# Two attention and mixture layers on one core: where one batch's shared expert and token sort stand among the next batch's attention units

## The chip, the cores and the metric

The kernel runs on one core of one Trainium2 chip. The core has a matrix engine (TensorE, PE in the profile, with its weight loads listed apart as PEld), a vector engine (VectorE, DVE), a scalar engine for activations (ScalarE, ACT), a general engine (GpSimd, POOL) and a queue engine (SyncE, SP) that issues most transfers. Each engine works through its own list of instructions in order and waits for the others by semaphores. The metric is the device time of one execution in microseconds (us); less is better.

## The reference, cut to what matters

Two batches `b` of 1,024 tokens with 128 channels go through two layers. Each layer adds an attention block and a mixture-of-experts block to the running sum `x`. All numbers are 32-bit floats. The change touches only the second layer's feed-forward block and its place beside the second layer's attention:

```python
logits = relu(xf @ Wr1 + br1) @ Wr2 + br2
tg, ti = top_k(softmax(logits), 2)
tg = softmax(tg / 2)
out = silu(xf @ Ws1 + bs1) @ Ws2 + bs2              # shared expert, every token
for e in range(8):                                  # routed experts
    h = silu(xf @ We1[e] + be1[e]) @ We2[e] + be2[e]
    w = sum(tg * (ti == e), axis=-1)
    out = out + w[:, None] * h
x = x + out
```

`xf` is the layer norm of `x` after the second attention. That attention is causal, with 16 heads of 8 channels, so a query tile with index `qt` (128 tokens) has only `(qt + 1) * 128` keys.

## The kernel before, in words

The first layer runs first, and then a short stretch in which the second layer's queries and keys of batch 0 are made. The second layer's attention is one loop over `N = 128` units `(b, qt, pr)`: batch, query tile, pair of heads. Units 0 to 63 are batch 0, units 64 to 127 batch 1, eight units (`pr`) to a query tile. In iteration `i` the loop issues, in this order: the scores of unit `i` (L1094 on PE; where this unit and the next are short, the scores and maxima of unit `i + 1` instead, one unit ahead), the transposes of the probabilities of `i - 1` (L1136), the exponentials of `i` (L1124 on ACT), the evictions of the transposes (L1142, on DVE and ACT), the product with the values for `i - 2` (L1175), at a tile's end the output projection (L1191), and then the side work. The negated maxima come from a DVE operation (L1102). A unit is short when it has at most 512 keys (`qt < 4`); its two heads then share one wide PSUM tile, and its maxima are taken in place. There are two wide PSUM tiles for scores, three banks (`bank()`) for everything else, and one accumulator.

PE, DVE, ACT and POOL keep the order in which the program issues, since this part is written under a manual schedule. So the place of a call in the loop is the place of its instructions in each engine's list.

The side work is written as generators that are advanced by one step at a time; a `yield` ends a step:

- `route1(b, t0, nt, ...)`, nine steps: statistics of the layer norm for `nt` tiles (L845, L846), the inverse root by a power on POOL (L108), one Newton step on DVE and four activations for the normed rows (L852), their transposes (L858), the copy to `lnT` (L859) and a write of the rows to `normed` in DRAM by SP, two router matmuls (L868, L873) with DVE operations between them, and three steps that pick the two largest gates (`picks`, small DVE operations).
- `send1(b, nt)`, twelve steps: the place of each token in an order sorted by expert, by prefix sums on PE and DVE (`places`), and then the token numbers for each sorted tile of 128 (`tokens_of`; sixteen accumulating matmuls at L357, a transpose at L363, and small DVE operations that end with the indices `s_id` at L375).
- `shared1(b, n)`, eight steps for 512 tokens, that is, two rounds of: a matmul of one quarter of the hidden width (L1056), its two activations (L1057 and the tanh L1059); the same for the next quarter, behind the DVE operation that ends the first (L1047); that operation for the second; eight products with the second weights (L1067) and the addition to `x` (L1069).
- `experts1(b, nt, early)`: the routed experts over sorted tiles. Its first step issues seven gathers on POOL (L923) by the indices of `send1`; the second asks for weights (L910, on SP); from the third on each step works on one tile (L962, L970, L975 on PE).

The list `side` holds pairs of a unit and a generator. `work(i)` advances the head of the list by one step, if its unit has come; a generator that has ended is dropped and the next one takes the step. The loop calls `work(i)` once at the end of each iteration, and once more from `last = 123` on. From unit 96 on, each odd iteration also advances `experts1` of batch 0. What is left of the list after the loop is done in the tail, with the rest of the experts, batch 1's shared expert and its own experts.

Of the kernel before, what the change touches and what calls it, by code (L numbers as in the profile page):

```python
# [23 lines left out]
NT = T // P  # L24
QB = 512
NQB = T // QB
TPB = QB // P
# [24 lines left out]
def two_layers(ctx, tc, a, out):  # L52
# [334 lines left out]
    with ExitStack() as st:  # L387
# [109 lines left out]
        N = len(units)  # L497
# [331 lines left out]
    def route1(b, t0, nt, tag_y, tag_n):  # L829


        if t0 == 0:
            y = a1.tile([P, T], F32, tag=tag_y, name="y1", bufs=1 if tag_y == "ckv" else 2)
            ys[b] = y.rearrange("p (t c) -> p t c", c=C)
            norms[b] = a1.tile([C, T], F32, tag=tag_n, name="lnT1", bufs=1 if tag_n == "lnT" else 2)
            gains[b] = small.tile([P, 2, NT], F32, tag="s_g", name="s_g", bufs=NB)
            hots[b] = small.tile([P, 2, NT, NE], F32, tag="s_h", name="s_h", bufs=NB)
        y, lnT = ys[b], norms[b]
        tiles = slice(t0, t0 + nt)
        cols = slice(t0 * P, (t0 + nt) * P)  # L840
        n = nt * P
        mv = small.tile([P, NT, 2], F32, tag="bnmv", name="bnmv", bufs=2)
        stats = small.tile([P, NT, 6], F32, tag="bnst", name="bnst", bufs=2)
        for t in range(t0, t0 + nt):
            nc.vector.bn_stats(stats[:, t, :], xs[b][:, t, :])  # L845
            nc.vector.bn_aggr(mv[:, t, :], stats[:, t, :])  # L846
        yield
        rstd = small.tile([P, NT], F32, tag="rstd", name="rstd", bufs=2)[:, tiles]
        yield from root(rstd, mv[:, tiles, 1], 2 if nt == 1 else 1)
        nm = shift(mv[:, tiles], rstd)  # L850
        for q in range(nt):
            nc.scalar.activation(y[:, t0 + q, :], xs[b][:, t0 + q, :], AF.Identity, bias=nm[:, q:q + 1],  # L852
                                 scale=rstd[:, q:q + 1])
        yield
        ps = bank()
        for q in range(nt):
            t = t0 + q
            nc.tensor.transpose(ps[:, q * P:(q + 1) * P], y[:, t, :], ident)  # L858
        nc.scalar.copy(lnT[:, cols], ps[:, :n])  # L859
        if nt > 1:  # L860
            nc.sync.dma_start(out=normed[b][t0 * P:(t0 + nt) * P, :].rearrange("(t p) c -> p t c", p=P),
                              in_=y[:, tiles, :])
        nc.gpsimd.tensor_tensor(xs[b][:, tiles, :], xs[b][:, tiles, :], bc(bs2.unsqueeze(1), [P, nt, C]), ALU.add)
        yield
        r1 = f1.tile([P, QB], F32, tag="r1", name="r1")
        nc.vector.memset(r1[32:33, :n], 1.0)
        ps = bank()
        nc.tensor.matmul(ps[:32, :n], wr1, lnT[:, cols], start=True, stop=True)  # L868
        nc.vector.tensor_scalar(r1[:32, :n], ps[:32, :n], br1, 0.0, ALU.add, ALU.max)
        yield  # L870
        ps = bank()
        for q in range(nt):
            nc.tensor.matmul(ps[:, q * NE:(q + 1) * NE], r1[:33, q * P:(q + 1) * P], wr2, start=True, stop=True)  # L873
        logits = small.tile([P, NT, NE], F32, tag="r_lg", name="r_lg", bufs=1)[:, :nt, :]
        nc.vector.tensor_copy(logits, ps[:, :nt * NE].rearrange("p (t e) -> p t e", e=NE))
        yield from picks(logits, nt, True, [hots[b][:, k, tiles, :] for k in range(2)],
                         [gains[b][:, k, tiles].unsqueeze(2) for k in range(2)])
        yield
# [193 lines left out]
    with ExitStack():  # L1072
        units = [(b, qt, pr) for b in range(NB) for qt in range(NT) for pr in range(8)]
        N = len(units)
# [121 lines left out]
        with tc.manual_schedule(engines={ET.PE, ET.DVE, ET.Activation, ET.Pool}):  # L1196
            steps = prepare(1)
            experts = experts1(0, NT, AHEAD)


            last = N // 2 + 8 * (NT - 1) + 3
            side = [(N // 2 + 3, route1(0, 0, TPB, "ckv", "lnT")), (0, route1(0, TPB, TPB, "ckv", "lnT")),
                    (0, send1(0, NT)), (0, shared1(0, 0)), (0, shared1(0, 1)),
                    (N // 2 + 8 * TPB + 3, route1(1, 0, TPB, "k0", "k1")),
                    (last, route1(1, TPB, 3, "k0", "k1")), (0, send1(1, NT - 1))]

            def work(i):

                while side and i >= side[0][0] and next(side[0][1], N) is not None:
                    side.pop(0)  # L1210

            issued = {}

            def issue(i):
                s = scores(i)
                issued[i] = maxima(i, s)

            for i in range(N + 3):
                ends = units[i - 1][:2] if 1 <= i <= N and units[i - 1][2] == 7 else None
                ahead = short(i) and short(i + 1)  # L1220
                if i < N and i not in issued:
                    if ahead:
                        issue(i)
                    else:
                        s = scores(i)
                if ahead:

                    issue(i + 1)
                if 1 <= i <= N:
                    probsT[i - 1] = a1.tile([P, 2 * NT, P], F32, tag="pT", name="pT", bufs=2)  # L1230
                    ps = fill(i - 1, 0)
                    if not short(i - 1):
                        for r in range(2):
                            evict(i - 1, 0, r, ps, nc.scalar.copy)
                if i < N:
                    if i in issued:
                        exponentials(i, *issued.pop(i))
                    else:
                        exponentials(i, *maxima(i, s))
                if 1 <= i <= N and short(i - 1):  # L1240
                    evict(i - 1, 0, 0, ps, nc.vector.tensor_copy)
                    evict(i - 1, 0, 1, ps, nc.scalar.copy)
                if ends:
                    recips[ends] = reciprocals(ends)
                if i >= last:
                    work(i)
                if 2 <= i <= N + 1:
                    values(i - 2)
                    if units[i - 2] == (0, NT - 1, 7):
                        spread_values(1)  # L1250
                if 1 <= i <= N and not short(i - 1):
                    ps = fill(i - 1, 1)
                    for r in range(2):
                        evict(i - 1, 1, r, ps, nc.vector.tensor_copy)
                probs.pop(i - 1, None)
                if i >= 3 and units[i - 3][2] == 7:
                    project_out(*units[i - 3][:2])
                work(i)
                if i >= N // 2 + 8 * TPB and i % 2:
                    next(experts, None)  # L1260
                if i < N:
                    b, qt, pr = units[i]

                    if b == 0 and qt >= 2 and (i % 2 or qt >= NT - 2) and (left > 6 or (qt, pr) >= (NT - 2, 3)):
                        next(steps, None)
                        left -= 1
                    if (b, qt, pr) == (0, NT - 1, 4):
                        for _ in steps:
                            pass
                    if qt + 1 < NT and pr == 0:  # L1270
                        mask_queries(b, qt + 1)
                    elif b + 1 < NB and (qt, pr) == (NT - 1, 5):
                        mask_queries(b + 1, 0)

            def run(*steps):

                return any([next(g, N) is None for g in steps])


            half, rest = shared1(1, 0), chain(route1(1, NT - 1, 1, "k0", "k1"), shared1(1, 1))  # L1280
            k = 0
            while side:
                work(N)
                if k % 2 == 0:
                    run(experts)
                run(rest)
                k += 1
            after = experts1(1, NT - 1, 1)
            for k in range(AHEAD):
                run(after)  # L1290
                run(half) if k % 2 else run(experts)
            while run(experts):
                run(after)
            combining = combine1(0, NT, 6)
            while run(after):
                run(half) or run(rest)
                run(combining)
            while run(half) or run(rest):
                pass
            dense, combining = all_experts1(1, NT - 1), combine1(1, NT - 1, 0)  # L1300
            while run(combining, dense):
                pass
            store(1, NT - 1, 1)
# [69 lines left out]
```

## Time and profile before

| what | value |
|---|---|
| median of three runs | 1475.38 us (1472.96 to 1479.55) |
| profiled execution | 1477.33 us, its span 1475.5 us |
| PE busy over the span | 1363.9 us (92%) |
| DVE, ACT, POOL busy | 1040.0 (70%), 905.2 (61%), 269.4 us (18%) |
| second attention, batch 0 (first exponential of unit 0 to that of unit 64) | 853.8 to 1055.5 us |
| batch 1, short units 64 to 95 | 1055.5 to 1148.5 us |
| batch 1, long units 96 to 119 | 1148.5 to 1280.1 us |
| units 120 to 127 and the tail | 1280.1 to 1475.5 us |

The table is read as follows. The profiled execution's own time is the span, in which its instructions lie, and 1.8 us around it. Busy times of engines overlap, so that they add up to far more than the span; what counts is which engine is busy nearly all the time in the stretch in question. The ends of matmuls are modelled. The stretches of the last four rows are cut at the first exponential (L1124) of a unit, found in the list of that line's instructions.

### The profile page before, as it was taken

What the parts mean: (1) busy time and instruction counts of PE and PEld (TensorE: products, weight loads), DVE (VectorE), ACT (ScalarE), POOL (GpSimd) and SP (SyncE); (2) the same over time, 40 slices, a digit from 0 to 9 for tenths busy, and PEclk for the clock granted to TensorE, in tenths of its full rate; (3) what the DMA queues carried; (4) which work ended last, traced back from release to release, by engine and by line L of the source; (5) the groups of instructions that cost most, each with busy time, mean ns of one, the idle gap of its engine ahead of it and who ended that gap; (6) DMA issues with size and microseconds to landing.
All of it is one profiled execution on the core that took longest, in us unless ns stands there. A gap on an engine that the chain in (4) does not pass through costs nothing.

```text
span 1475.5 us, 40490 instructions
## 1 busy us (share of the span) xinstructions
PE 1363.9 (92%) x16931; PEld 981.6 (67%) x16931; DVE 1040.0 (70%) x2376; ACT 905.2 (61%) x1915; POOL 269.4 (18%) x246
## 2 busy tenths in 40 slices
PE   5999999999999999999998989999987899987787
PEld 2777777777777776777765555666654577756676
DVE  3787767777766868777457478678879467877476
ACT  3778567777755776776422267867666577753443
POOL 1010010000000100000154641011021212213553
PEclk9999999999999999999999989999999999999999
DMA  4000000000000000000110030000000011112453
GB/s 111 2 16 17 16 2 17 16 16 17 16 16 2 16 16 16 17 16 2 31 35 1 0 92 2 2 2 2 2 16 30 16 30 34 50 30 66 140 128 112
DMA packets 31319, 43.15 MB, mean 29 GB/s; under 512 B 7545, under 2 KB 19506, under 8 KB 31138
## 3 DMA queue, kind: packets, MB, share of 16 engines
q1 hardware_dynamic: 25216, 28.47, 7.0%
q0 software_dynamic: 4352, 10.70, 2.8%
q8 instruction: 134, 2.20, 0.6%
q10 hardware_dynamic: 1570, 1.41, 0.4%
q14 instruction: 47, 0.39, 0.1%
HBM read 35.51 MB, written 5.05 MB: 27 GB/s over the span
## 4 chain that ended last, share of the span: by engine, by line
PE 77%; DVE 12%; ACT 6%; issue 4%; DMA 1%; another core or an unknown queue 0%; POOL 0%; DVEq 0%; POOLq 0%; SPq 0%; ACTq 0%
PE ps_s L507 16%; PE ps_a L574 16%; PE ps_t L557 10%; PE ps_s L1094 8%; PE ps_t L1136 4%; PE ps_s L253 3%; PE ps_a L1175 3%; DVE ps_s L1102 2%; PE ps_a L492 2%; PE ps_t L970 2%; PE ps_t L962 2%; PE ps_t L591 2%; ACT p L1124 2%; PE ps_t L728 2%; PE ps_t L263 2%
## 5 line engine op out<-in xcount | busy, mean ns | idle before, releaser
L516 DVE CUSTOM_DVE_ANT_0 p<-ps_s,zero 128x1024 f32<-128x1024 f32 x256 | 303.4, 1222 | 122.9 <-PE ps_s L507 121.8
L526 ACT ACTIVATE p<-p,nmx 128x1024 f32<-128x1024 f32 x256 | 293.1, 1153 | 6.7 <-DVE nmx L516 6.7
L563 ACT COPY pT<-ps_t 128x512 f32<-128x512 f32 x256 | 137.5, 589 | 199.3 <-PE ps_t L557 199.3
L507 PE MATMUL ps_s<-qk 64*128 64x512 f32 x1024 | 252.2, 607 | 1.5 <-DVE nmx L516 1.4
L574 PE MATMUL ps_a<-pT,zv 128*64 128x128 f32 x4096 | 251.8, 276 | 0.0
L574 PEld LDWEIGHTS ps_a<-pT,zv 128*64 128x64 f32 x4096 | 220.9, 137 | 9.3 <-issue 0.8
L557 PEld LDWEIGHTS ps_t<-ident,p 64*128 64x128 f32 x4096 | 160.3, 139 | 89.8 <-issue 85.9
L563 DVE COPY pT<-ps_t 128x512 f32<-128x512 f32 x256 | 164.9, 686 | 45.3 <-PE ps_t L557 43.1
L1094 PE MATMUL ps_s<-k,qm 64*128 64x512 f32 (+3 forms) x768 | 170.7, 533 | 13.6 <-ACT p L1124 11.2
L557 PE MATMUL ps_t<-ident,p 64*128 64x64 f32 x4096 | 178.1, 226 | 1.3 <-DVE pT L563 0.7
L1102 DVE CUSTOM_DVE_ANT_0 p<-ps_s,cmask 128x640 f32<-128x640 f32 (+3 forms) x128 | 126.0, 1022 | 71.2 <-PE ps_s L1094 60.8
L548 POOL TENSOR_TENSOR aoT<-aoT,recip 128x1024 f32<-128x1024 f32 x16 | 37.9, 2368 | 656.6 <-DMA recip<-flat 481.7
L507 PEld LDWEIGHTS ps_s<-qk 64*128 64x128 f32 x1024 | 93.2, 189 | 83.7 <-issue 74.7
L1142 ACT COPY pT<-ps_t 128x512 f32<-128x512 f32 (+3 forms) x192 | 95.7, 533 | 76.2 <-PE ps_t L1136 71.0
L1136 PEld LDWEIGHTS ps_t<-ident,p 64*128 64x128 f32 x2304 | 104.7, 140 | 55.6 <-issue 28.1
L1124 ACT ACTIVATE p<-p,nmx 128x640 f32<-128x640 f32 (+3 forms) x128 | 125.9, 992 | 4.5 <-DVE nmx L1102 4.5
L1136 PE MATMUL ps_t<-ident,p 64*128 64x64 f32 x2304 | 118.6, 228 | 9.3 <-issue 4.0
L1094 PEld LDWEIGHTS ps_s<-k,qm 64*128 64x128 f32 x768 | 71.7, 193 | 79.7 <-issue 43.6
L1175 PE MATMUL ps_a<-pT,vx 128*32 128x128 f32 x2304 | 98.3, 279 | 11.1 <-DVE pT L1142 10.2
L1142 DVE COPY pT<-ps_t 128x128 f32<-128x128 f32 (+3 forms) x192 | 87.3, 482 | 9.6 <-PE ps_t L1191 6.0
L1124 ACT ACTIVATE p<-ps_s,nmx 128x128 f32<-128x128 f32 (+3 forms) x128 | 66.3, 524 | 35.5 <-DVE nmx L1102 34.6
L899 ACT ACTIVATE th<-h 128x512 f32<-128x512 f32 x52 | 32.8, 630 | 87.9 <-DVE h L896 72.7
(255 smaller groups left out, 1817.2 us busy)
## 6 DMA issues: line engine op xcount, KB each, us to landing
we<-in_we SPq DMA_DIRECT2D x52, 256.0 KB
recip<-flat SPq DMA_DIRECT2D x32, 256.0 KB
we<-in_we POOLq DMA_DIRECT2D x1, 2048.0 KB
z<-results SPq DMA_DIRECT2D x6, 256.0 KB
x<-in_x SPq DMA_DIRECT2D x4, 256.0 KB
up<-in_up_proj POOLq DMA_DIRECT2D x1, 1024.0 KB
normed<-y SPq DMA_DIRECT2D x3, 256.0 KB
out_x<-x SPq DMA_DIRECT2D x3, 256.0 KB
```

The costliest lines, as they stand in the source:

```text
L507: nc.tensor.matmul(s[h][:, n * QB:(n + 1) * QB], qk[rows, 0, qt * P:(qt + 1) * P], qk[rows, 1, n * QB:(n + 1) * QB], start=True, stop=True)
L516: nc.vector.tensor_tensor_reduce(p, s, bc(zero, [P, T]), -1.0, 3e38, ALU.add, ALU.min, nmx)
L526: nc.scalar.activation(p, p, AF.Exp, bias=nmx, scale=-1.0, accum_out=ssum[:, h, qt:qt + 1])
L557: nc.tensor.transpose(ps[r][:, k * 64:(k + 1) * 64], probs[i][h][rows, k * P:(k + 1) * P], ident[rows, rows])
L563: copy(probsT[i][h][:, :, r * 64:(r + 1) * 64], ps[r].rearrange("p (j q) -> p j q", q=64))
L574: nc.tensor.matmul(acc[h * D0:(h + 1) * D0, cols], zv[:, j, :], probsT[i][h][:, j, :], start=(j == 0), stop=(j == NT - 1))
L1094: nc.tensor.matmul(s[h][:, n * QB:n * QB + w], qms[b, qt][rows, pr, :], kTs[b][pr // 4][rows, n * QB:n * QB + w], start=True, stop=True)
L1102: nc.vector.tensor_tensor_reduce(to[:, :nk], s[:, :nk], cmask[:, T - nk:], -1.0, 3e38, ALU.add, ALU.min, nmx)
L1124: nc.scalar.activation(p[:, h, :nk], s[h][:, :nk], AF.Exp, bias=nmx[h], scale=-1.0, accum_out=sums[b, qt][:, head:head + 1])
L1136: nc.tensor.transpose(ps[r][:, c * 64:(c + 1) * 64], probs[i][rows, h, j * P:(j + 1) * P], ident[rows, rows])
L1142: copy(probsT[i][:, 8 * f:8 * f + n, r * 64:(r + 1) * 64], ps[r][:, :n * 64].rearrange("p (j q) -> p j q", q=64))
L1175: nc.tensor.matmul(acc[to * 32:(to + 1) * 32, k * P:(k + 1) * P], vx[:, j, g, pr % 4 * 24:pr % 4 * 24 + 32], probsT[i][:, h * (qt + 1) + j ...
```

## The change

Two edits are made. In the list `side`, the two `shared1` of batch 0 move from behind `send1(0, NT)` to between and behind the two `route1` of batch 0, so that each half of the shared expert follows the routing of its own 512 tokens, and `send1` comes last of the five. And in iterations 64 to 95 each odd one calls `work(i)` a second time, so that three side steps are issued in two units, and not two.

```diff
-            side = [(N // 2 + 3, route1(0, 0, TPB, "ckv", "lnT")), (0, route1(0, TPB, TPB, "ckv", "lnT")),
-                    (0, send1(0, NT)), (0, shared1(0, 0)), (0, shared1(0, 1)),
+            side = [(N // 2 + 3, route1(0, 0, TPB, "ckv", "lnT")), (0, shared1(0, 0)),
+                    (0, route1(0, TPB, TPB, "ckv", "lnT")), (0, shared1(0, 1)), (0, send1(0, NT)),
                     (N // 2 + 8 * TPB + 3, route1(1, 0, TPB, "k0", "k1")),
                     (last, route1(1, TPB, 3, "k0", "k1")), (0, send1(1, NT - 1))]
...
                 work(i)
+                if N // 2 <= i < N // 2 + 8 * TPB and i % 2:
+                    work(i)
                 if i >= N // 2 + 8 * TPB and i % 2:
                     next(experts, None)
```

`NT` is 8 (tiles of 128 tokens in a batch) and `TPB` is 4 (tiles in 512 tokens), so `N // 2 + 8 * TPB` is 96 and `N // 2 + 8 * TPB + 3` is 99. No operation is added or taken away, and no buffer changes its size.

## The prediction

> **What bounds the kernel now.** I number the units of the second attention by the loop's `i`: batch 1 begins at 64, its short rows (128 to 512 keys) are 64 to 95, its long rows 96 to 127. The view of engine time by stretch comes first, cut where a unit's first exponential starts: batch 0's short units, batch 0's units 48 to 55, batch 1's short units (call it stage A), then batch 1's units 96 to 103 and 104 to 111 (together stage B), and 112 to 119.
>
> ```profile
> core 0: us, PE busy (x) PEld busy (x) DVE busy (x) ACT busy (x) POOL busy (x), PEclk, DMA share, GB/s
> 853.80:919.50 65.70, 58.63 (x776) 38.15 (x776) 52.09 (x192) 49.04 (x171) 17.85 (x25) 0.92 0.19 52
> 981.50:1020.90 39.40, 39.15 (x526) 23.58 (x522) 30.21 (x61) 25.24 (x51) 7.12 (x6) 1.00 0.01 2
> 1055.50:1148.50 93.00, 72.94 (x915) 48.29 (x911) 76.07 (x292) 52.00 (x183) 13.17 (x12) 0.96 0.06 19
> 1148.50:1191.90 43.40, 36.37 (x428) 23.52 (x424) 23.03 (x65) 28.48 (x64) 12.95 (x13) 0.92 0.09 24
> 1191.90:1235.50 43.60, 42.92 (x553) 31.20 (x552) 30.26 (x70) 32.13 (x70) 5.97 (x6) 1.00 0.11 32
> 1235.50:1280.10 44.60, 44.18 (x616) 33.17 (x614) 37.09 (x93) 31.66 (x70) 11.47 (x11) 1.00 0.15 45
> ```
>
> See PE: busy 72.94 of 93.0 us (0.78) in A, but 0.98 and 0.99 in the 44 us stretches from 1191.9 on. The chain of waits, asked for these stretches, says the same: adding up its listed pieces, A's chain lies 45.1 us on DVE and 24.3 on PE, B's 66.0 us on PE and 4.6 on DVE. So PE work taken out of B should shorten it; PE work put into A meets 20 us of idle PE, but behind DVE. Next the timeline of units 97 and 98, where B's first stretch falls to 0.84:
>
> ```profile
> 1153.94 1.12 PE L1056 MATMUL ps_t<-lnT,ws 128*128 128x512 f32 x2 [0.98 <-DVE recip L1182]
> ...
> 1160.95 1.07 ACT L1142 COPY pT<-ps_t 128x512 f32<-128x512 f32 x2 [4.59 <-remote]
> ...
> 1161.59 0.47 PE L1136 MATMUL ps_t<-ident,p 64*128 64x64 f32 x3 [3.77 <-issue]
> ...
> 1164.30 2.08 PE L1056 MATMUL ps_t<-lnT,ws 128*128 128x512 f32 x2 [1.00 <-DVE pT L1142]
> ```
>
> ACT stands 4.59 us before a copy whose matmuls had ended at 1156.84; PE then waits 3.77 us for the bank that this copy frees. All this lies inside seven gathers that POOL issues from 1152.36 to 1162.26. Afterwards the same pair of L1056 takes 2.08 us, not 1.12: from 1162.0 to 1168.5 the granted clock is 0.53. Cost by parts: 3.77 + 6.5 x (1 - 0.53) = 6.8; by units: 97 and 98 take 17.25 us between first exponentials, the neighbours 96 and 100 4.34 and 5.04, so 17.25 - 9.0 = 8.2. I take 7.5.
>
> **The change, part by part.** Before, one side step goes behind each unit from 67: nine of the first `route1`, nine of the second, twelve of `send1`, ending at 96, then batch 0's two `shared1` at 97 to 112. After, odd units up to 95 take two: 44 steps by 95, 46 by 97. Steps 1-9 are `route1` (67 to 72), 10-17 `shared1` (73 to 77), 18-26 `route1` (78 to 83), 27-34 `shared1` (84 to 89), 35-46 `send1` (89 to 97). Nothing is computed more or less.
>
> *What moves*: sixteen shared steps leave B for A. Their groups, of which batch 0 is half:
>
> ```profile
> L1056 PE MATMUL ps_t<-lnT,ws 128*128 128x512 f32 x32 | 19.4, 691 | 6.8 <-DVE x L1069 4.4 <-DVE pT L1142 1.0 <-DVE recip L1182 1.0
> L1067 PE MATMUL ps_t<-ws,hs 128*128 128x128 f32 x128 | 16.0, 278 | 0.3 <-ACT pT L1142 0.2
> L1067 PEld LDWEIGHTS ps_t<-ws,hs 128*128 128x128 f32 x128 | 14.9, 192 | 0.9 <-ACT pT L1142 0.9
> L1047 DVE SCALAR_TENSOR_TENSOR hs<-ths,hs 128x512 f32<-128x512 f32 x16 | 11.1, 693 | 0.0
> L1057 ACT ACTIVATE hs<-ps_t,bs 128x512 f32<-128x512 f32 x16 | 11.0, 686 | 4.9 <-PE ps_t L1056 4.1 <-issue 0.5
> ```
>
> PE: eight pairs of L1056 at 1.18 us (592 ns each at full clock) and four blocks of sixteen L1067 at 2.05 (1173.52 in the timeline) = 9.4 + 8.2 = 17.6 us. ACT: L1057 5.5 and L1059 5.5 = 11.0. DVE: L1047 5.5 and four L1069 at 0.69 = 8.3.
>
> *B without them*: -17.6 us. PE is left with about 58 us there (36.4 + 42.9 - 17.6, less the 3 us that the slow clock added), ACT with 60.6 - 11.0 = 49.6, DVE with 53.3 - 8.3 = 45, so PE stays the longest. "Perfetto Trace Analysis" of the Trainium skill (Identifying the Most-Contended Engine) speaks against this step: matmul busy time doesn't tell how loaded PE is, weight-load busy time does. By it B is loaded 0.54 and 0.72, the shared steps weigh (5.2 + 14.9) / 2 = 10.1 us (5.2 is L1056's own loads), and the sum below ends at -0.9. The trace settles it: from batch 0's units 48 to 55 to the same rows of batch 1 (39.40 us at 981.5, 44.60 at 1235.5; other side work stands there) the stretch grows 5.2 us, busy matmul 5.0, weight loads 9.6. The stretch follows matmul time; I take 17.6, and 10.1 as the weak end.
>
> *A with them*: the trace of before shows no shared step beside a short unit, so both ends. Best: PE 72.94 + 17.6 = 90.5 at the occupancy that batch 0's short units reach (58.63 / 65.70 = 0.89) gives 101.7, +8.7. Worst: nothing overlaps, PE, ACT and DVE parts add in full, 17.6 + 11.0 + 8.3 = +36.9. Between: the eleven units that carry shared steps are PE's. A short unit has 58.63 / 32 = 1.83 us of PE, so 20.1 + 17.6 = 37.7, at 0.95 (in paired steps the halving add L1047 stands at DVE's head until its tanh is there, and L1067 waits for that add) 39.7. The eighteen with `route1` and `send1` are DVE's: 52.09 / 32 = 1.63 us each, 29.3, and the steps' own 76.07 - 52.09 = 24.0, less one step, 23.2: 52.5 at A's own 0.82 is 64. Units 64 to 66: 6. Sum 109.7, **+16.7**. So I expect nearly no gain from A's idle PE, because the DVE steps that make it idle stand in other units than the matmuls.
>
> The weights that the shared steps need were asked at 858 to 859 us and the DMA is all but idle again by 890, so starting them at 73 waits for no transfer.
>
> *Two steps in one unit*: at 69 the wr1 matmul waits in PE's queue for the copy of `lnT` just asked of ACT, with the next scores behind it; at 79 the Newton step waits at DVE's head for POOL's power (1.0 us, row of L108), with the next maxima behind; at 81 the second router matmul waits for DVE. About 1 us each, held by the 0.82; below nothing if the pairs save a semaphore turn.
>
> *`send1` behind it*: the indices come one unit later (97, not 96), the gathers too. What needs them is the first expert transpose at 101: 0, at most +2. SP's gather source, `normed`, is written at 80 as before at 79.
>
> *Batch 1's first `route1`*: 113-121 before, 99-107 after (unit 98 has nothing due). PE about 4 us in either place (half of L858, L868, L873 in A), both at 0.98: 0, within 2. Its `normed` write passes ahead of five expert weight loads on SP's queue; its power stands behind seven gathers on POOL (1.25 us apart), done some 13 us after unit 97 starts, before 101 asks. 108 to 122 stay without a side step. From 123 on nothing moves.
>
> *The stall at 97*: ACT had run 1,725 instructions (its sequencer's counted). The 8,192-byte deliveries on the queue q14 `instruction` near ACT's earlier ones fall at counts 1213, 1341 and 1597, each a multiple of 128 from the others, and 1725 lies 128 behind the last; so ACT changed its code block in the midst of the gathers. After, sixteen more activations stand ahead of 97, the change comes about two units earlier, before the first gather, and the stall goes: -7.5. "Runtime: NRT & Kernel Launch" (Instruction fetch mechanics) says the opposite: crossing a block costs one tail bump, mostly hidden. Then the gathers alone stopped ACT and stop it again: 0. I go by the counts. With the stall gone, what is late next is PE itself.
>
> **Sum**: +16.7 - 17.6 - 7.5 = -8.4 us. The profiled execution took 1477.33 (span 1475.5 and 1.8 around it), 1.95 above the median 1475.38 of three; taken off that median: **1467**.
>
> **Rivals.** *The stall recurs*, or another engine's block change meets the gathers: -0.9, 1474.5. For: the burst is still there; against: the counts. *A absorbs*: +8.7 in place of +16.7, 1459. For: PE idle 20 us; against: A's chain on DVE. *Slower: ACT's and DVE's heads in the short units.* L1057 and L1059 stand in ACT's order ahead of the next unit's exponentials and must wait for L1056 behind the side matmuls; short units have two wide banks, so scores can run one unit ahead only. In A the list of waits has PE's loads for the scores standing for an exponential 9.5 us already, in 15 waits. If all of the 19.3 us of ACT and DVE work lies open: +36.9 - 17.6 - 7.5 = +11.8, **1487**; it outweighs the gains from 39% open ((25.1 - 17.6) / 19.3). Against: in B the same order leaves PE at 0.98. That the change doesn't do what it says is out: the built order has all sixteen steps ahead of unit 90.
>
> **Numbers.** Forecast 0.45 (its own range 1461 to 1472), stall recurs 0.23, A absorbs 0.12, slower 0.20. What a measurement tells from no change is 0.5%, 7.4 us. Faster: 0.12 + 0.45 x 0.7 = 0.44. Same: the rest of the forecast, most of the recurring stall and part of the slower case, 0.34. Slower 0.22. The range, 1455 to 1486, takes in all four but the outer tails.
>
> **What would show it.** Right: A near 110 us, PE about 0.83; B near 62, PE over 0.95, no ACT gap of 4 us and the clock at 1.0; unit 123 reached 8 us earlier. Wrong: A over 118, with ACT gaps before exponentials and PE stopped at L1094; B under 12 us shorter; a 4 us gap anew.

## The result and the profile after

The changed kernel takes **1489.47 us** (median of four, 1486.0 to 1491.99) where the kernel before takes 1476.64 (four runs, 1472.96 to 1479.55): ratio **1.0088, 95% interval 1.0061 to 1.0116**. The forecast was 1467, 0.6% faster. The profiled execution took 1486.0, its span 1484.2.

The view of engine time by stretch, cut at the same units as the one in the prediction: units 64 to 95 (stage A), 96 to 103 and 104 to 111 (stage B), 112 to 119.

```profile
core 0: us, PE busy (x) PEld busy (x) DVE busy (x) ACT busy (x) POOL busy (x), PEclk, DMA share, GB/s
1049.90:1167.50 117.60, 95.15 (x961) 60.36 (x958) 85.65 (x304) 61.19 (x198) 13.41 (x12) 0.83 0.05 15
1167.50:1208.50 41.00, 34.51 (x447) 24.66 (x438) 23.18 (x75) 25.73 (x62) 15.06 (x15) 0.92 0.12 32
1208.50:1247.50 39.00, 36.54 (x522) 28.42 (x522) 30.46 (x85) 27.40 (x64) 5.98 (x6) 1.00 0.11 36
1247.50:1288.80 41.30, 41.09 (x587) 30.76 (x585) 31.60 (x65) 29.60 (x63) 8.89 (x9) 1.00 0.14 42
```

A grew from 93.0 to 117.6 us, by 24.6 where 16.7 were forecast. B went from 87.0 to 80.0, by 7.0 where 25.1 were forecast, and PE is still free for 9 us of it. The last stretch gave 3.3: the last shared matmuls (unit 112) and batch 1's first `route1` have moved out of it. The shared steps cost PE the same as before: over the whole execution the L1056 matmuls take 18.9 us (19.4 before) and L1067 takes 16.5 (16.0).

A's list of groups shows where new waits stand. First the kernel before, then the changed one; the figures after the bar are busy us, mean ns of one, then the engine's idle time ahead of the group and who ended it.

```profile
L852 ACT ACTIVATE y<-x,shift,rstd 128x128 f32<-128x128 f32 x8 | 3.3, 482 | 2.5 <-DVE shift L119 2.5
L858 PE MATMUL ps_t<-ident,y 128*128 128x128 f32 x8 | 2.9, 402 | 1.5 <-ACT y L852 1.3
L869 DVE TENSOR_SCALAR r<-ps_t,br 32x512 f32<-32x512 f32 x2 | 1.5, 739 | 0.2 <-PE ps_t L868 0.2
```

```profile
L1047 DVE SCALAR_TENSOR_TENSOR hs<-ths,hs 128x512 f32<-128x512 f32 x8 | 6.0, 749 | 4.8 <-ACT ths L1059 4.8
L852 ACT ACTIVATE y<-x,shift,rstd 128x128 f32<-128x128 f32 x8 | 3.3, 482 | 7.3 <-DVE shift L119 7.3
L858 PE MATMUL ps_t<-ident,y 128*128 128x128 f32 x8 | 3.3, 475 | 3.5 <-ACT y L852 3.5
L1069 DVE SCALAR_TENSOR_TENSOR x<-ps_t,x 128x512 f32<-128x512 f32 x4 | 2.8, 692 | 4.1 <-PE ps_t L1067 4.1
L869 DVE TENSOR_SCALAR r<-ps_t,br 32x512 f32<-32x512 f32 x2 | 1.5, 739 | 3.9 <-PE ps_t L868 3.9
```

These are the same operations with the same durations, but each now stands at the head of its engine and waits for a result that was asked for just ahead of it: 4.8 us more at L852, 2.0 at L858, 3.7 at L869, and 8.9 new ones on DVE at the shared expert's L1047 and L1069.

The timeline at unit 98 shows the stop that the forecast had taken away:

```profile
1176.84 1.07 ACT L1142 COPY pT<-ps_t 128x512 f32<-128x512 f32 x2 [0.87 <-PE ps_t L1136]
1177.21 1.09 POOL L923 DMA_INDIRECT back<-normed,s_id  x1 [18.09 <-DVE s_id L375]
...
1179.79 0.66 PE L1136 MATMUL ps_t<-ident,p 64*128 64x64 f32 x16
...
1183.64 0.95 POOL L923 DMA_INDIRECT back<-normed,s_id  x1 [0.30 <-issue]
1184.89 0.95 POOL L923 DMA_INDIRECT back<-normed,s_id  x1 [0.30 <-issue]
1185.99 1.07 ACT L1142 COPY pT<-ps_t 128x512 f32<-128x512 f32 x2 [6.46 <-remote]
1186.63 0.47 PE L1136 MATMUL ps_t<-ident,p 64*128 64x64 f32 x3 [4.44 <-ACT pT L1142]
```

The copy on ACT needs the sixteen transposes that ended at 1180.45. It begins at 1185.99, just after the last of the seven gathers (1184.89 + 0.95 = 1185.84), and PE stands 4.44 us behind it. In the kernel before, ACT was let go at 1160.95, and the seventh of eight gathers (the forecast had counted seven up to 1162.26) ended at 1161.00; DVE stood 6.00 us at its own copy (L1142), until 1163.95. A second profile of the changed kernel has the same stop (6.40 and 4.39 us). In a second profile of the kernel before, ACT is let go after 3.20 us, during the sixth gather, and DVE stands 5.98 us.

### The profile page after: what moved, and what is told of

Read it like the earlier page. It is cut to its first block, busy times and chain, and to the rows that moved or that the text cites. A ratio compares the mean times of both kernels' runs of the same rounds, so it can differ in the third digit from the quotient of the medians.

```text
span 1484.2 us, 40479 instructions
## 1 busy us (share of the span) xinstructions
PE 1369.4 (92%) x16931; PEld 987.6 (67%) x16931; DVE 1042.5 (70%) x2376; ACT 904.9 (61%) x1915; POOL 268.6 (18%) x246
## 4 chain that ended last, share of the span: by engine, by line
PE 76%; DVE 11%; ACT 7%; issue 4%; another core or an unknown queue 1%; DMA 1%; POOL 0%; DVEq 0%; ACTq 0%; POOLq 0%; SPq 0%
PE ps_s L507 15%; PE ps_a L574 15%; PE ps_t L557 10%; PE ps_s L1094 8%; PE ps_t L1136 4%; PE ps_s L253 3%; PE ps_a L1175 3%; DVE ps_s L1102 2%; ACT p L1124 2%; PE ps_a L492 2%; PE ps_t L591 2%; PE ps_t L962 2%; PE ps_t L728 2%; PE ps_t L263 2%; PE ps_t L970 2%
## 5 line engine op out<-in xcount | busy, mean ns | idle before, releaser
L557 PEld LDWEIGHTS ps_t<-ident,p 64*128 64x128 f32 x4096 | 159.3, 139 | 89.1 <-issue 85.3
L563 DVE COPY pT<-ps_t 128x512 f32<-128x512 f32 x256 | 164.8, 685 | 44.4 <-PE ps_t L557 42.1
L1094 PE MATMUL ps_s<-k,qm 64*128 64x512 f32 (+3 forms) x768 | 173.2, 537 | 11.7 <-ACT p L1124 10.0
L557 PE MATMUL ps_t<-ident,p 64*128 64x64 f32 x4096 | 177.0, 225 | 1.3 <-DVE pT L563 0.7
L1142 ACT COPY pT<-ps_t 128x512 f32<-128x512 f32 (+3 forms) x192 | 96.0, 535 | 86.0 <-PE ps_t L1136 79.0
L1136 PEld LDWEIGHTS ps_t<-ident,p 64*128 64x128 f32 x2304 | 109.1, 144 | 56.7 <-issue 25.2
L1136 PE MATMUL ps_t<-ident,p 64*128 64x64 f32 x2304 | 123.9, 232 | 9.5 <-ACT pT L1142 6.1
L1094 PEld LDWEIGHTS ps_s<-k,qm 64*128 64x128 f32 x768 | 74.2, 195 | 75.0 <-issue 40.2
L1175 PE MATMUL ps_a<-pT,vx 128*32 128x128 f32 x2304 | 101.7, 284 | 13.6 <-DVE pT L1142 12.6
L1142 DVE COPY pT<-ps_t 128x128 f32<-128x128 f32 (+3 forms) x192 | 87.2, 482 | 12.8 <-PE ps_t L1136 12.4
```

The lines of the kernel that those rows point to most:

```text
L557: nc.tensor.transpose(ps[r][:, k * 64:(k + 1) * 64], probs[i][h][rows, k * P:(k + 1) * P], ident[rows, rows])
L563: copy(probsT[i][h][:, :, r * 64:(r + 1) * 64], ps[r].rearrange("p (j q) -> p j q", q=64))
L1094: nc.tensor.matmul(s[h][:, n * QB:n * QB + w], qms[b, qt][rows, pr, :], kTs[b][pr // 4][rows, n * QB:n * QB + w], start=True, stop=True)
L1136: nc.tensor.transpose(ps[r][:, c * 64:(c + 1) * 64], probs[i][rows, h, j * P:(j + 1) * P], ident[rows, rows])
L1142: copy(probsT[i][:, 8 * f:8 * f + n, r * 64:(r + 1) * 64], ps[r][:, :n * 64].rearrange("p (j q) -> p j q", q=64))
L1175: nc.tensor.matmul(acc[to * 32:(to + 1) * 32, k * P:(k + 1) * P], vx[:, j, g, pr % 4 * 24:pr % 4 * 24 + 32], probsT[i][:, h * (qt + 1) + j ...
```

## The experiments

Each kernel was compared with the kernel before on its own chip. Two chips served; on the second every kernel ran some 28 us faster (the kernel before 1447.05 there, about 1475 on the first), so only ratios and stretches are compared across them. Stretches are cut at the first exponential of a unit, in the profiled execution, and take in both units named; "half" is the time in which the granted clock was about 0.5.

| kernel | ratio (95%) | units 64-96 (half) | 97-103 | 104-122 |
|---|---|---|---|---|
| before, two profiles | 1 | 97.3 (6.8), 96.9 (13.7) | 39.1, 38.8 | 104.1, 104.2 |
| changed, two profiles | 1.0088, 1.0087 (1.0063-1.0111) | 124.3 (41.0), 126.1 (37.5) | 34.3, 34.3 | 96.0, 96.0 |
| single_routes | 1.007 (1.005-1.0091) | 119.8 (23.9) | 35.0 | 97.3 |
| after_warm | 1.0144 (1.0124-1.0164) | 128.9 (30.7) | 34.4 | 95.9 |
| before_gathers_apart | 0.9988 (0.9976-0.9999) | 99.8 (23.9) | 35.7 | 106.2 |
| pairs_alone, second chip | 1.0039 (1.0029-1.005) | 106.0 (41.0) | 30.8 | 103.5 |
| pairs_even, second chip | 1.0081 (1.0049-1.0112) | 107.3 (44.4) | 30.8 | 103.5 |
| after_spread, second chip | 1.0092 (1.006-1.0125) | 125.3 (41.0) | 25.9 | 96.5 |
| after_spread_again, first chip | 1.0077 (1.0048-1.0106) | 125.3 (41.0) | 29.3 | 97.9 |
| beside | 0.9978 (0.9963-0.9994) | 108.1 (13.7) | 34.1 | 95.9 |
| beside_spread, second chip | 0.9998 (0.9981-1.0016) | 107.7 (13.7) | 28.8 | 96.3 |
| beside_spread_again, first chip | 0.9955 (0.9939-0.9972) | 108.0 (13.7) | 29.3 | 97.6 |

### Is it the two steps in one unit, or the shared expert in short rows?

**The changed order, with single steps of the routing and the sort, and the shared expert in four packs.** Each `shared1` runs four steps in a unit, in units 76, 77, 87 and 88; the experts' odd units start at 101.

```diff
+            packed = (N // 2 + 12, N // 2 + 13, N // 2 + 23, N // 2 + 24)
...
-                if N // 2 <= i < N // 2 + 8 * TPB and i % 2:
-                    work(i)
-                if i >= N // 2 + 8 * TPB and i % 2:
+                if i in packed:
+                    for _ in range(3):
+                        work(i)
+                if i > N // 2 + 8 * TPB + 4 and (i % 2 or i < N // 2 + 8 * TPB + 10):
```

> The order of the changed kernel, but the steps of route1 and send1 stand one to a unit as before, and each shared1 is put whole into two units (four steps each, units 76, 77, 87, 88); send1 then ends at unit 100 and the routed experts begin at 101 and catch up by 109. Theory A (two DVE-heavy steps in one unit leave PE idle, and the granted clock halves): in units 64 to 100 the clock is halved for about 7 us, as before the change, not 41 us; the total is 8 to 12 us under the changed kernel, 1.001 to 1.004 of before. Theory B (shared1's matmuls and activations in short units cost this by themselves, at the heads of ACT's and DVE's queues): the total stays at 1.008 or above, as four shared steps in one unit are denser still.

Units 64 to 96 took 119.8 us, and the kernel stayed slower. The waits of `route1` went back to those of before (L869 0.2 us, L852 3.0), but those of the shared expert grew (L1047 6.3, L1069 9.1). So the pairs of routing steps are not the whole cause: shared steps in units of their own cost 22 us here, although four steps of `send1` had moved out behind unit 96. They stand four to a unit, as a chain of dependent steps; one to a unit, without other side work beside them, was not tried. Neither forecast came whole: the total was above the 1.004 of theory A and just under the 1.008 of theory B, and the half-clock time 23.9 us, not 7.

**The second step alone.** The list of before, with the second step in odd units up to 95 and the shared expert held back to unit 97, where it was.

```diff
-                    (0, send1(0, NT)), (0, shared1(0, 0)), (0, shared1(0, 1)),
+                    (0, send1(0, NT)), (N // 2 + 33, shared1(0, 0)), (0, shared1(0, 1)),
...
                 work(i)
+                if N // 2 <= i < N // 2 + 8 * TPB and i % 2:
+                    work(i)
```

> The kernel before, with the second step in each odd unit from 65 to 95 alone: route1, route1 and send1 end at unit 86 in place of 96, and batch 0's shared1 stays at units 97 to 112. Theory P (two dependent steps in one unit cost extra, whatever stands there): units 64 to 95 last 100 to 106 us, not 93.0, the clock is halved for more than 20 us of them, and the total is 1.004 to 1.009 of before. Theory S (the extra time of the changed kernel comes from shared1 in the short units, not from the pairs): units 64 to 95 last 90 to 95 us and the total is within 0.002 of before.

Units 64 to 96 took 106.0 us, 8.7 more than before: nothing was added, yet the thirty steps took 72.3 us in the twenty units 67 to 86, the ten units then left bare 26.4, and together 98.7 where the thirty units had taken 90.1 with one step each.

The extra lies in the routing. Its two `route1` took 20.8 and 22.6 us in six units each, where nine units had taken 22.9 and 24.8; `send1` took 28.9 us in eight units where twelve had taken 42.4. Batch 0's units of the same rows give a rough measure of what the units cost without these steps (an estimate from the profile of before, since other side work stands in some of them): over it the two `route1` cost 22.7 us here and 13.4 before, `send1` 11.3 and 10.6. The groups of units 64 to 95 show the waits:

```profile
L868 PE MATMUL ps_t<-lnT,wr 128*32 128x512 f32 x4 | 3.8, 1061 | 2.0 <-ACT lnT L859 2.0
L852 ACT ACTIVATE y<-x,shift,rstd 128x128 f32<-128x128 f32 x8 | 3.3, 481 | 6.5 <-DVE shift L119 6.5
L858 PE MATMUL ps_t<-ident,y 128*128 128x128 f32 x8 | 3.3, 475 | 2.0 <-ACT y L852 2.0
L869 DVE TENSOR_SCALAR r<-ps_t,br 32x512 f32<-32x512 f32 x2 | 1.5, 738 | 6.9 <-PE ps_t L868 6.9
```

**The same in even units.** Which two steps share a unit might matter, since in the changed kernel the second `route1` pairs a power on POOL with the Newton step that reads it, and one router matmul with the next. The edit is that of the run above with `i % 2 == 0`.

> The earlier run with the second step alone (in odd units 65 to 95) took 106.0 us over units 64 to 96 where the kernel before takes 97.3. Here the same second step stands in the even units 68 to 94, and nothing else differs. If any two steps in one unit cost the same, whichever they are, these units take 106 us again. If it is steps that depend on each other (in even units the pairs of the first and second route1 fall so that a step that raises a power on POOL and the Newton step on DVE that reads it, and a router matmul and the next, stand in one unit; in odd units of the earlier run they did not), they take 111 to 116 us.

Units 64 to 96 took 107.3 us: which steps are paired hardly matters. The waits only change places, as the same groups of this kernel show.

```profile
L852 ACT ACTIVATE y<-x,shift,rstd 128x128 f32<-128x128 f32 x8 | 3.3, 482 | 8.4 <-DVE shift L119 8.4
L858 PE MATMUL ps_t<-ident,y 128*128 128x128 f32 x8 | 3.3, 474 | 4.2 <-ACT y L852 4.2
L873 PE MATMUL ps_t<-wr,r 33*128 33x8 f32 x16 | 2.9, 304 | 1.8 <-DVE r L869 0.9 <-issue 0.9
L869 DVE TENSOR_SCALAR r<-ps_t,br 32x512 f32<-32x512 f32 x2 | 1.5, 738 | 0.9 <-PE ps_t L868 0.9
```

From 6.9 us at L869, the wait has gone to L852 and L858. (The two kernels' ratios differ by 0.4% although units 64 to 122 differ by 1.3 us only; in the profiles the rest lies ahead of unit 64, where the programs are the same, and behind 122.)

**The shared expert beside the routing.** Here the list keeps single steps, and each odd unit from 71 gets one shared step beside its routing or sorting step. `tile_hot` of `send1` gets a buffer of its own, as its slot was that of `hs`.

```diff
-        tile_hot = a1.tile([P, 2 * QB], F32, tag="hs", name="hot")[...]
+        tile_hot = a1.tile([P, 2 * QB], F32, tag="hot", name="hot")[...]
...
-                    (0, send1(0, NT)), (0, shared1(0, 0)), (0, shared1(0, 1)),
+                    (0, send1(0, NT)),
...
+            beside = chain(shared1(0, 0), shared1(0, 1))
...
                 work(i)
...
+                if N // 2 + 7 <= i and i % 2:
+                    next(beside, None)
```

> The list and the single steps of the kernel before, but batch 0's shared1 is taken out of the list and advanced by one step in each odd unit from 71 to 101, so that its matmuls share units with the DVE steps of route1 and send1 (the hot tile of send1 gets a buffer of its own). Theory A: the clock in units 64 to 95 is halved for 7 us or less, the short units last 100 to 106 us (93.0 before, 117.6 after), and the total is 0.990 to 0.999 of before. Theory B: the short units last 112 us or more, and the total is 1.005 or above.

Units 64 to 96 took 108.1 us with thirteen of the sixteen shared steps in them, and the kernel became faster than before, by 0.2% (95% interval 0.06 to 0.37). Its groups in units 64 to 95:

```profile
L1047 DVE SCALAR_TENSOR_TENSOR hs<-ths,hs 128x512 f32<-128x512 f32 x6 | 4.1, 684 | 0.0
L852 ACT ACTIVATE y<-x,shift,rstd 128x128 f32<-128x128 f32 x8 | 3.3, 481 | 2.8 <-DVE shift L119 2.8
L1069 DVE SCALAR_TENSOR_TENSOR x<-ps_t,x 128x512 f32<-128x512 f32 x3 | 2.1, 689 | 1.6 <-PE ps_t L1067 1.6
L869 DVE TENSOR_SCALAR r<-ps_t,br 32x512 f32<-32x512 f32 x2 | 1.5, 738 | 0.2 <-PE ps_t L868 0.2
```

Two steps share a unit here too, but they belong to two chains that don't depend on each other. The wait at L1047 is 0.0 where it was 4.8, and the routing's waits are close to those of the kernel before (2.8 and 0.2 us, 2.5 and 0.2 there).

### Is it the clock?

The clock stood at one half for 41 us of units 64 to 96 after the change, for 6.8 before. PE's work there is stretched by it: 95.15 us are busy in units 64 to 95 where 72.94 + 17.6 - 3.7 (L357 had moved to unit 96) = 86.8 were due.

**More work for PE.** The changed kernel, with the transposes of the probabilities (L1136) of batch 1's short units done twice.

```diff
-            for c, (h, j) in enumerate(blocks(i)[8 * f:8 * f + 8]):
+            for _ in range(2 if N // 2 <= i < N // 2 + 8 * TPB else 1):
+                for c, (h, j) in enumerate(blocks(i)[8 * f:8 * f + 8]):
...
```

> The changed kernel, with every transpose of the probabilities of batch 1's short units issued twice into the same place, some 15 us more of PE work without a wait of its own. Theory A (the halved clock is what costs): the clock in units 64 to 95 rises from 0.83 to 0.95 or more, and the total is no longer than that of the changed kernel, in spite of the work. Theory B (the clock only follows idle time that other waits make, and costs nothing): the short units last 8 to 15 us longer than the 117.6 us of the changed kernel.

The half-clock time only fell to 30.7 us, and the stretch grew to 128.9. Neither theory's figure came: the clock in units 64 to 95 rose to 0.88, not 0.95, and these units became 3.4 us longer, not 8 to 15, with 6.1 us more of busy PE. The stronger witness is the program of units 64 to 96 of before, which stands unchanged in three profiles (the third is that of before_gathers_apart, below): its half-clock time was 6.8, 13.7 and 23.9 us, its stretch 97.3, 96.9 and 99.8 us. From the first to the second a halved us costs nothing, from the first to the third 0.15 us, from the second to the third 0.28. At such rates, which are estimates from single profiles, the 41 - 7 us after the change would explain between nothing and 10 us of the 27. So the clock is not the whole cause, and its share stays open.

### What stops ACT at unit 97 or 98?

The forecast had put the stop down to a change of ACT's code block in the midst of the gathers. In the changed kernel the instruction delivery fell at 1163.95, when ACT had run 1,723 instructions, and the stop began at 1179.5, 15.6 us later, with ACT at 1,747. In the kernel before, the delivery itself fell at 1162.18, when ACT had already been let go. So that theory had fallen before any experiment. Nor does a delivery on the other queue of instructions, q8, make the stop by itself: there is one at 1177.00, just ahead of the first gather, and none from there to the stop's end; with the gathers held apart (below) one stands just as close (1182.84, first gather 1182.96), and there is no stop. What was left was the burst of gathers.

**The gathers one by one, in the kernel before.** `experts1` was told to issue one gather for each step, one step to a unit.

```diff
-            experts = experts1(0, NT, AHEAD)
+            experts = experts1(0, NT, 1)
...
-                if i >= N // 2 + 8 * TPB and i % 2:
+                if i >= N // 2 + 8 * TPB + 1 and (i % 2 or i < N // 2 + 8 * TPB + 14):
```

> The kernel before, with the seven first gathers of batch 0's routed experts issued one to a unit in units 97 to 103 and not all at 97; the experts' steps then go one to a unit up to 109, where they have caught up. Theory G (the burst of gathers holds up ACT's wait for PE): no gap over 3 us on ACT before L1142, the granted clock 1.0 in units 96 to 103, and 5 to 9 us less in all, 0.994 to 0.997. Theory C (it is ACT's change of code block that meets a gather, which is where I put it in the prediction): ACT's gap of 4 us stays, or moves, and the total is within 2 us of before.

The edit failed to do what it was for: nothing made POOL wait between the gathers, so that it ran ahead of the units and issued them 1.26 us apart as ever. The stop was there (3.21 us on ACT, 4.63 on DVE), and the run says nothing of the burst.

**The gathers held apart, in the changed kernel.** Ahead of each gather POOL adds two columns of the unit's maxima, and so has to wait for that unit.

```diff
-            experts = experts1(0, NT, AHEAD)
+            experts = experts1(0, NT, 1)
...
+                if N // 2 + 8 * TPB < i < N // 2 + 8 * TPB + 8:
+                    pace = small.tile([P, 1], F32, tag="pace", name="pace", bufs=1)
+                    nc.gpsimd.tensor_tensor(pace, moved[1][0], moved[1][0], ALU.add)
+                if i >= N // 2 + 8 * TPB + 1 and (i % 2 or i < N // 2 + 8 * TPB + 14):
...
```

> The changed kernel, with the seven first gathers held apart in time: ahead of each, in units 97 to 103, POOL adds up two columns that DVE writes in that unit, so that it cannot run ahead (in before_gathers_apart nothing held it, and the gathers still came 1.26 us apart). Theory G (the burst of gathers holds up what waits for PE): no gap over 2.5 us on ACT or PE in units 97 to 103, the clock 1.0 there, and 5 to 9 us less than the changed kernel, 1.003 to 1.006 of before. Rival: each gather holds up PE's release by itself, and seven small gaps take the place of the large one; the total is within 2 us of the changed kernel's.

> The changed kernel with the gathers held apart by POOL. Theory G: units 97 to 103 last 26 us on any chip; where after_again has its stop, 7 to 9 us less than after_again, where it has none, the same.

> The changed kernel, once more, on the same chip as its neighbours here. Units 64 to 96 last 124 us as before on either kind of chip (theory P: pairs and shared1 cost 27 us there). Units 97 to 103 last 34 us where the gathers stop PE, 26 to 27 where they do not; in the second case the total is still 1.007 to 1.010 of before, as before loses its own stop too.

> The kernel before, once more, for a profile on the same chip as the next three. If the stop at units 97 and 98 belongs to the burst of gathers on every chip: units 97 to 103 last about 39 us and ACT stands over 4 us before L1142. If it belongs to the chip of the first two calls, as pairs_alone suggests (the same burst, 30.8 us, no stop, on a chip where all kernels are 28 us faster): units 97 to 103 last 31 to 33 us wherever the total is near 1447 us, and 39 us wherever it is near 1475 us.

The first of these runs was on the second chip; the others are on the first, with both kernels unchanged among them. Its timeline there, at the same units:

```profile
1182.96 1.10 POOL L923 DMA_INDIRECT back<-normed,s_id  x1 [3.45 <-DVE s_id L375]
...
1184.46 0.98 POOL L923 DMA_INDIRECT back<-normed,s_id  x1 [0.16 <-issue]
...
1186.30 1.07 ACT L1142 COPY pT<-ps_t 128x512 f32<-128x512 f32 x2 [1.00 <-PE ps_t L1136]
...
1187.61 0.96 POOL L923 DMA_INDIRECT back<-normed,s_id  x1 [0.45 <-issue]
...
1189.53 1.07 ACT L1142 COPY pT<-ps_t 128x512 f32<-128x512 f32 x2 [0.54 <-PE ps_t L1136]
```

With 1.4 us and more from one gather to the next, ACT waits 1.00 us where it stood 6.46, and unit 98 takes 3.69 us in place of 9.16. Units 97 to 103 are 5.0 us shorter, but 104 to 122 are 1.9 longer, and the medians (1487.38 against 1488.72) don't tell the two apart; both held-apart runs of this order missed the totals expected of them (1.003 to 1.006 of before on the second chip, 7 to 9 us less than the changed kernel on the first). So, in this order and on this chip, the burst is needed for the stop, and the stop is worth 5 us where it stands; how much of it reaches the end can't be told.

The stop is not ACT's alone. In single_routes, on the first chip, the burst stands four units later, and there DVE waits for transposes that had ended at 1186.52, until 1.6 us after the last gather:

```profile
1186.19 0.33 PE L1136 MATMUL ps_t<-ident,p 64*128 64x64 f32 x3 [1.00 <-DVE nmx L1102]
...
1188.82 0.95 POOL L923 DMA_INDIRECT back<-normed,s_id  x1 [0.30 <-issue]
1191.34 0.49 DVE L1142 COPY pT<-ps_t 128x128 f32<-128x128 f32 x2 [5.56 <-remote]
```

In beside it is DVE again (4.70 us, until 1.5 us after the last gather). So every profile of a burst on the first chip has such a stop, on ACT, on DVE or on both.

On the second chip pairs_alone and pairs_even issued their gathers in a burst too, 1.25 us apart but from 6.7 us ahead of unit 97 on, and have no stop: units 97 and 98 of pairs_alone took 9.2 us, those of the kernel before 17.25 and 17.0 in its two profiles. Whether the chip or the earlier place of the burst makes that difference was not tried apart, and why ACT and DVE are let go so late after PE's matmuls in a burst stays open.

**Both together.** The shared expert beside the routing, and the gathers held apart: the edits of beside and after_spread in one kernel.

> The kernel beside, with the gathers held apart in the same way. Theory G: 3 to 8 us less than beside, 0.992 to 0.996 of before. Rival: the same as beside, 0.998.

> shared1 beside route1 and send1, and the gathers held apart. Where before has the stop: 0.991 to 0.996 of before. Where it has none: 0.998 to 1.001, as in the run on the faster chip.

On the first chip it took 1468.12 us where the kernel before took 1475.08, ratio 0.9955 (0.9939 to 0.9972): the best of all, and faster than both kernels. On the second chip it is even with before (0.9998), under the 0.992 to 0.996 that were expected; that the kernel before has no stop there would explain it, but no profile of it was taken on that chip. Its gain over beside (0.9978) is within the two intervals.

## Why the prediction was wrong

Between units 64 and 122 the forecast's sum was -8.4 us, and the profiles have 254.6 - 240.5 = +14.1 (in the profiled execution 5.6 of it was hidden, as unit 64 began earlier). The difference of 22.5 us divides by the forecast's own terms so:

- **The eighteen units with routing and sorting, 64 us.** They took 20.8 (units 67 to 72), 27.7 (78 to 83) and 27.2 (90 to 95), 75.7 in all: **11.7 more. This is the step that failed**: "52.5 at A's own 0.82 is 64", with two steps in one unit at "about 1 us each, held by the 0.82". It divided A's busy time by an occupancy that holds with one step to a unit. The first `route1` took 22.9 us in nine units before and 20.8 in six after, the second 24.8 and 27.7: its nine dependent steps last 21 to 28 us, in six units as in nine, and the units taken from them are paid for elsewhere. By the measure of batch 0's units (an estimate, as above) the two `route1` cost 25.3 us over their units where they had cost 13.4, `send1`'s steps in 90 to 95 10.4 where its twelve had cost 10.6: the miss lies in the routing, and for `send1` the division held. pairs_alone and pairs_even show it without the shared expert: 8.7 and 10.0 us. How much of these is the lower clock that goes with the pairs stays open (half-clock time of 30.7 to 44.4 us in every profile with pairs, 6.8 to 23.9 without). The waits themselves are hardly the clock's: L852 waits for DVE's shift, and the L868 matmuls ahead of L869 only grew from 826 to 1061 ns. The forecast had named these waits (lnT, the power, the second router matmul), and had them hidden.
- **The eleven units with shared steps, 39.7 us.** They took 15.88 + 18.87 = 34.75, 5.0 less. The forecast was right that the shared expert finds little idle PE in units of its own: PE was busy for 0.89 and 0.86 of them, and for 0.75 to 0.77 of those with routing and sorting. But A's idle PE can be had: beside puts thirteen steps (seven pairs of L1056 and three blocks of L1067, 14.4 us of PE by the forecast's pieces) there for 10.8 us more, as neighbours of DVE's steps.
- **Units 64 to 66, 6 us**: 7.2.
- **`send1` one unit later, "0, at most +2"**: unit 96 took 6.6 us in place of 4.3, as `send1`'s sixteen L357 matmuls (3.7 us, two records each in the profile) now stand in it: 2.3, just over the end given.
- **The stall gone, -7.5.** It came again. Its size was about right (units 97 and 98 took 17.25 us with it, 9.2 in pairs_alone without, on the other chip), its cause wrong: "I go by the counts" was the mistake, an argument from three deliveries. At the delivery at 1163.95 no stop is seen; ACT's next wait, 3.11 us, is for DVE's maxima. "Runtime: NRT & Kernel Launch" of the Trainium skill (Instruction fetch mechanics), which says that crossing a block is mostly hidden, was right for this crossing. After the change the stop costs 9.16 - 3.69 = 5.5 us, before some 7.9, so this term is -2.4, and 5.1 were missed.
- **B without the shared steps, -17.6.** Units 97 to 122 became 12.8 us shorter, 10.4 without the 2.4 of the stop. Without a stop on either side, on the second chip, pairs_alone to after_spread gives (30.8 + 103.5) - (25.9 + 96.5) = 11.9. So 7.2 were missed. Where they went shows in the units one by one. Units 104 to 111 lost 8.6 us of shared matmuls and became only 4.6 shorter. They took 5.25, 6.04, 4.99, 5.36, 5.25, 6.76, 4.32 and 5.57 us before, and 4.16, 6.56, 3.91, 5.62, 3.39, 6.36, 3.39 and 5.57 after. The even ones lost 6.3 us of these matmuls and gave 5.0, with a step of batch 1's `route1` now in 104. Of the odd ones, in which a step of the experts runs, only 105 and 109 had such matmuls (2.2 us), and the two together gave nothing: PE now stands 1.17 us for DVE's L896 in 105, and 0.73 us for a copy of ACT in 109. In units 99 to 103, 4.3 us of matmuls went out, but the five became only 0.3 shorter: unit 99, behind the stop, became 1.5 longer, and batch 1's `route1` came in. Where it had stood, units 113 to 121 gave 2.1 back, so that for its own move the forecast's 0 is plausible, though no run shows it apart. The measure by weight loads that the forecast had set aside, from "Perfetto Trace Analysis" of the Trainium skill (Identifying the Most-Contended Engine), gave -10.1, nearer than the busy time. That is in part luck, as a sum over units of which some gave most of their matmul time and others nothing. The row that was used against it (5.2 us between two stretches of batch 0 and batch 1) compared stretches in which PE was 0.99 busy; it says nothing of units that an expert's step sets.

These make 11.7 - 5.0 + 1.2 + 2.3 + 5.1 + 7.2 = 22.5.

Of the rivals, the slower one had the right sign and almost the place (1487), by luck, for its price was put on L1057 and L1059 standing ahead of the exponentials. ACT's idle ahead of L1057 is 6.4 us in A, but the exponentials' own fell from 19.6 to 14.3; the time went to the paired chains, to the stop that stayed and to what B did not give. "A absorbs" was out, "the stall recurs" was true, and by itself too small. Of the signs named for "wrong", A over 118 came (117.6 and 119.3 in the two profiles), B 7.0 shorter, and a gap of 6.46 us; longer gaps ahead of the exponentials and PE stopped at L1094 did not (4.7 us of idle, 7.0 before).

## What to carry to other kernels

A chain of small steps that wait for each other across engines, like `route1`, takes its latency, not its busy time: putting two of its steps into one unit hardly shortens it, and gives away the units that covered it. Fill its gaps with steps of another, independent chain on another engine instead; here that won 0.2%. Work taken out of a stage is worth its busy time only in those units where its engine sets the end; look at the units one by one, and leave out those whose end another step sets anyway. And before a stall is counted as gone, show with one run that it goes when its supposed cause goes.

## What the runs showed of the hardware

- While POOL issued seven or eight indirect gathers 1.26 us apart, on the first chip, ACT or DVE was let go up to 5.5 us after the matmuls that it waited for had ended. ACT was let go about the end of the seventh gather in three profiles of the changed order (6.46, 6.40 and, in after_warm, 6.46 us of idle ACT) and in one of the kernel before (4.59), during the sixth in two of the order before (3.20 and 3.21). DVE stood 4.6 to 6.0 us in all three profiles of the order before, in single_routes and in beside. With the gathers held apart (1.4 us and more) ACT waited 1.00 us at the same units, and 2.1 at most up to unit 103. Two bursts on the second chip, placed earlier, made no such stop.
- Gathers that wait for nothing run ahead: placed one to a unit in the program, they still issued 1.26 us apart.
- The half-clock time of one and the same program stretch was 6.8, 13.7 and 23.9 us in three profiles, with the stretch at 97.3, 96.9 and 99.8 us. By these a halved us cost between nothing and 0.28 us, where PE was busy for 0.78 to 0.83 of units 64 to 95.
- Up to unit 64's start, where nearly all the programs are the same, the profiles differ by up to 10.8 us (1044.72 to 1055.52), more than some effects that were looked for. So stretches between two marks were compared, and whole times by medians only.
- Two chips differ by 28 us for the same kernel, and 20 of them lie behind unit 122 (159 to 162 us there, 178 to 183 on the first).
